# Second attention of a two-layer AdaLN kernel: projections at 0.6 to 0.8 of a round, its elementwise steps in the last fifth

## The chip, the cores and the metric

The kernel runs on one core of a Trainium2 chip. The metric is the device time of one execution in microseconds (us); the time before is 2012.13 us, the median of three runs (2011.39 to 2016.81). One further execution was profiled.

The engines are written as in the profile: PE (TensorE, matrix products; PEld are its weight loads), DVE (VectorE), ACT (ScalarE), POOL (GpSimd), SP (SyncE, which here only starts DMAs). Each engine works off its own queue in order.

## What is computed

The input is 8 sequences of 512 tokens with 128 channels. Two layers follow, each of an attention part and a feed-forward part, with layer norms, scales and gates from a condition vector. Shortened:

```python
h = layernorm(x) * (1 + ca) + sa
x = x + ga * L0_attn(h)        # 16-head causal attention and a state space scan, mixed; then a dense FFN
h = layernorm(x) * (1 + cb) + sb
x = x + gb * L0_ffn(h)         # 8 experts, 2 per token, and a shared one
h = layernorm(x) * (1 + ca) + sa
x = x + ga * L1_attn(h)        # "second attention"
h = layernorm(x) * (1 + cb) + sb
x = x + gb * L1_ffn(h)         # channel mix with the token before
```

The state space scan of layer 0 runs over 512 tokens for 256 channels and 16 states each: `h = exp(dt*A)*h + (x*dt)*B`, `y = sum_n C*h`.

The second attention (`L1_attn`) gets its axes swapped: what it treats as the sequence is the batch of 8, so that each token position attends over the 8 sequences, in 8 heads of 16 channels, without a mask. A window of 65 is padded with zeros, which adds 57 zero scores to each softmax sum:

```python
q = (x @ Wq.T + bq) * scale;  k = x @ Wk.T + bk;  v = x @ Wv.T + bv
scores[i, j, h] = sum_d q[i, h, d] * k[j, h, d]      # i, j over the 8, for each position
probs = softmax(scores with 57 zeros added)
out[i] = sum_j probs[i, j, h] * v[j]
```

## The kernel before

**Rounds.** `for b in range(NB)` (line 1285) makes eight rounds. Each traces several generators, "parts", interleaved by `weave`. A part is `(pieces, whole, begin, end)`: its pieces yield a cost, `whole` is the sum of its costs, and `weave` always advances the part whose place is lowest, where a part starts at `begin` and moves by `cost * (end - begin) / whole`. The numbers 0 to 1 are thus places in the order of one round and not times. The loop stands in a manual schedule for PE, ACT and DVE: these three engines issue in the order in which the pieces are traced. POOL and SP are ordered by the scheduler.

The parts of round b are: the rest of attention b of layer 0 (`ahead`, 0 to 1), the scan of b (`ssm_scan`, 0 to 0.83), the norm of b+1 (`head`, 0.1 to 0.55), the second attention of b-2 (`attention2`, 0 to 1, from b = 2 on), the scan's inputs for b+1 (`after`, 0.8 to 0.97), the first pieces of attention b+1 (0.85 to 1), and the FFN, routing and experts of b-1 (`behind`, 0 to 0.9). After the last round the second attention of sequences 6 and 7 runs beside the channel mix of layer 1.

**The scan** (`ssm_scan`, line 770). Sixteen units, two states by 128 channels each. DVE multiplies the input (L815), runs two scans (L820) and adds the two states (L804, in the first two units L799); POOL multiplies each scan's result by C (L823) and adds to the sum (L805, L802), in the end times the gate (L834). ACT makes the decays (L790) and starts the loads of B and C (L783). Then PE projects (L839) and DVE adds (L846).

**The scan's inputs** (`ssm_inputs`, line 684). PE L688 and L709, a convolution on DVE (L697), silu on ACT, PE L724, then for each half of the channels: PE L742, ACT L750, L751, L753, POOL L755, DVE L758, POOL L759; then ACT L765, POOL L766 and L767.

**The second attention** (`attention2`, line 316). A layer norm (`lnc` tiles: PE L256, ACT L259 and L261, PE L268, DVE L277, POOL's power at L278, PE L283, DVE L290, ACT L297). Four `kv` tiles (PE L329, two DVE sums L338 each) and one `q` tile (PE L347, DVE L354). Token positions lie on the partitions, so the rest is elementwise: in `attended` (line 360), for each of four query pairs, POOL multiplies k by q in two halves (`pr`, L377) and DVE sums over the channels (L366). DVE takes the maximum and subtracts it (L391 to L393), ACT takes two exponentials (L395, L396), DVE makes the softmax (L398 to L403). Then POOL multiplies v by the weights (`pv`, L417), DVE sums over the 8 (L408), and SP stores the result (`kept`, L432). `pr`, `pv` and the normalised input share one ring of two buffers; `k2`, `v2` and `q2` have one buffer each.

`attention2` ends with `yield from paced(attended(...))`: `paced` traces each piece so that its instructions queue behind the last marked DVE instruction of the layer 0 attention.

All the products of PE that are not attention scores or sums take their PSUM tile from one ring of three buffers (`mm_tile`, line 155).

**Other lines used below.** L544 row maxima of layer 0 attention (DVE); L563 adds them to q; L623, L635 its normalisation; L652 (ACT) and L653 (POOL) add one half of its result to h, L655 (DVE) the other; L478 its values; L582 its exponentials. Experts: L1128 gathers rows (POOL DMA), L1185 and L1211 their two products (PE), L1222 and L1223 store, L1234 gathers the results (POOL DMA), L1246, L1251, L1259, L1262 add them to x.

Of the kernel before, what the change touches and what calls it, by code (L numbers as in the profile page):

```python
# [19 lines left out]
NB = 8  # L20
# [56 lines left out]
def kernel(  # L77
# [51 lines left out]
    def crow(name):  # L129
        a, b = ROW[name]  # L130
        return row_sb[:, a:b]
# [23 lines left out]
    def mm_tile(name):  # L155
        return pmm.tile([P, 512], F32, tag="mm", name=name)
# [34 lines left out]
    def mod(l, j, b):  # L191
        return mods[l][:, j, b : b + 1]
# [35 lines left out]
    def paced(pieces):  # L228

        pieces, cost = iter(pieces), 0.0  # L230
        while cost is not None:
            if marks:
                with tc.issue_after(marks[0]):
                    cost = next(pieces, None)
            else:
                cost = next(pieces, None)
            if cost is not None:
                yield cost
# [55 lines left out]
    def layernorm(dst, src, scale, bias, name, lane, cost=0.9, n=T, ring=mm_tile, wait=0.0):  # L294

        d = yield from normalised(src, name, lane, cost, n, ring, wait)
        nc.scalar.activation(dst, d, AF.Identity, bias=bias, scale=scale)  # L297
        yield cost
# [10 lines left out]
    def cwb(name):  # L309
        lo, hi = WB[name]  # L310
        return wb_sb[:, lo:hi]

    def half(k):
        return slice(U * k, U * k + U)

    def attention2(s, at):

        hT = at.tile([P, 2, T], F32, tag="pr", name=f"hT{s}", bufs=2)[:, 0, :]
        yield from layernorm(hT, xT[:, s, :], mod(1, 1, s), mod(1, 0, s), f"lnc{s}", SECOND)

        k2 = at.tile([P, NB, C], F32, tag="k2", name=f"k2_{s}", bufs=1)
        v2 = at.tile([P, C, NB], F32, tag="v2", name=f"v2_{s}", bufs=1)
        q = at.tile([P, NQ, C], F32, tag="q2", name=f"q2_{s}", bufs=1)
        bias = crow("qkv_b").unsqueeze(1)
        for i0 in range(0, NB, 2):
            ps = mm_tile(f"kv{s}_{i0}")
            for i in range(2):
                for k in range(2):
                    nc.tensor.matmul(  # L329
                        ps[half(k), 2 * C * i : 2 * C * (i + 1)],  # L330
                        lhsT=hT[:, (i0 + i) * U : (i0 + i + 1) * U],
                        rhs=cwb("qkv")[:, C:],
                        start=True,
                        stop=True,
                    )
            both = k2, v2.rearrange("p c i -> p i c")
            for k, to in enumerate(t[:, i0 : i0 + 2, :] for t in both):
                nc.vector.tensor_add(  # L338
                    to,
                    ps.rearrange("p (i k c) -> p k i c", i=2, k=2)[:, k],  # L340
                    bias[:, :, C * (k + 1) : C * (k + 2)].to_broadcast([P, 2, C]),
                )
            yield 0.9
        ps = mm_tile(f"q2{s}")
        for i in range(NQ):
            for k in range(2):
                nc.tensor.matmul(  # L347
                    ps[half(k), C * i : C * (i + 1)],
                    lhsT=hT[:, (NQ * k + i) * U : (NQ * k + i + 1) * U],
                    rhs=cwb("qkv")[:, :C],  # L350
                    start=True,
                    stop=True,
                )
        nc.vector.tensor_add(  # L354
            q, ps.rearrange("p (i c) -> p i c", i=NQ), bias[:, :, :C].to_broadcast([P, NQ, C])
        )
        yield 0.9
        yield from paced(attended(s, at, q, k2, v2))

    def attended(s, at, q, k2, v2):  # L360

        sc = at.tile([P, NQ, NB, H1], F32, tag="sc", name=f"sc{s}", bufs=1)

        def summed(last):
            i, pr = last
            nc.vector.tensor_reduce(  # L366
                sc[:, i, :, :].rearrange("p j h -> p (j h)"),
                pr.rearrange("p j (h d) -> p (j h) d", d=D1),
                AX.X,
                ALU.add,  # L370
            )

        last = None
        for i in range(NQ):
            pr = at.tile([P, NB, C], F32, tag="pr", name=f"pr{s}_{i}", bufs=2)
            for k in range(0, NB, NQ):
                nc.gpsimd.tensor_mul(  # L377
                    pr[:, k : k + NQ, :],
                    k2[:, k : k + NQ, :],
                    q[:, i, :].unsqueeze(1).to_broadcast([P, NQ, C]),  # L380
                )
            if last:
                summed(last)
            last = i, pr
            yield 1.6
        summed(last)

        scale = float(D1) ** -0.5
        s3 = [P, NQ, NB, H1]
        mx = at.tile([P, NQ, H1], F32, tag="mx", name=f"mx{s}", bufs=1)  # L390
        nc.vector.tensor_reduce(mx, sc.rearrange("p i j h -> p i h j"), AX.X, ALU.max)  # L391
        nc.vector.tensor_scalar(mx, mx, 0.0, None, ALU.max)
        nc.vector.tensor_sub(sc, sc, mx.unsqueeze(2).to_broadcast(s3))  # L393
        yield 1.6
        nc.scalar.activation(sc, sc, AF.Exp, scale=scale)  # L395
        nc.scalar.activation(mx, mx, AF.Exp, scale=-scale)  # L396
        sm = at.tile([P, NQ, H1], F32, tag="sm", name=f"sm{s}", bufs=1)
        nc.vector.tensor_reduce(sm, sc.rearrange("p i j h -> p i h j"), AX.X, ALU.add)  # L398
        nc.vector.scalar_tensor_tensor(
            sm, mx, float(PADS), sm, op0=ALU.mult, op1=ALU.add  # L400
        )
        nc.vector.reciprocal(sm, sm)
        nc.vector.tensor_mul(sc, sc, sm.unsqueeze(2).to_broadcast(s3))  # L403
        ao = at.tile([P, NQ, C], F32, tag="ao", name=f"ao1_{s}", bufs=1)

        def gathered(last):
            i, pr = last
            nc.vector.tensor_reduce(ao[:, i, :], pr, AX.X, ALU.add)  # L408

        last = None  # L410
        for i in range(NQ):
            pr = at.tile([P, C, NB], F32, tag="pr", name=f"pv{s}_{i}", bufs=2)
            HH = H1 // 2
            s4 = [P, HH, D1, NB]
            for k in range(2):
                cs, hs = (slice(k * n, (k + 1) * n) for n in (C // 2, HH))
                nc.gpsimd.tensor_mul(  # L417
                    pr[:, cs, :].rearrange("p (h d) j -> p h d j", d=D1),
                    v2[:, cs, :].rearrange("p (h d) j -> p h d j", d=D1),
                    sc[:, i, :, hs].rearrange("p j h -> p h j").unsqueeze(2).to_broadcast(s4),  # L420
                )
            if last:
                gathered(last)
            last = i, pr
            yield 1.6
        gathered(last)
        if s == NB - 1:
            at2.append(ao)
            return
        kept = dram.tile([NB, U, C], F32, tag=f"ao{s}", name=f"kept{s}", bufs=1)  # L430
        for k in range(2):
            nc.sync.dma_start(  # L432
                out=kept[NQ * k : NQ * (k + 1)].rearrange("i u c -> u i c"), in_=ao[half(k)]
            )
        at2.append(kept)
# [10 lines left out]
    with ExitStack() as l0:  # L446
# [6 lines left out]
        a2 = l0.enter_context(tc.tile_pool(name="a2", bufs=2))  # L453
# [655 lines left out]
        def experts(b, hm, hmd, rt, ei, pos, tw, wT):  # L1109
# [154 lines left out]
            )  # L1264
            yield 2.4

        ready, inputs, routed = {}, {}, {}
        nc.sync.dma_start(out=wb_sb, in_=wb)

# [13 lines left out]
        with tc.manual_schedule(engines={mybir.EngineType.PE, mybir.EngineType.Activation, mybir.EngineType.DVE}):  # L1283
            behind = None
            for b in range(NB):
                h = ready[b][0]


                parts = [(ahead, 48.1, 0.0, 1.0)]
                parts.append((paced(ssm_scan(b, h, *inputs.pop(b))), 19.3, 0.0, 0.83))  # L1290
                if b + 1 < NB:
                    parts.append((head(b + 1), 9.5, 0.1, 0.55))
                if b >= 2:
                    parts.append((attention2(b - 2, a2), 23.4, 0.0, 1.0))
                if b + 1 < NB:
                    parts.append((after(b + 1), 8.0, 0.8, 0.97))
                    ahead = attention(b + 1)
                    parts.append((some(ahead, BEGUN), 7.3, 0.85, 1.0))
                if behind:
                    parts.append((behind, 88.8, 0.0, 0.9))  # L1300
                weave(*parts)
                behind = finish(b, h)
# [9 lines left out]
            LAST = NB - 1  # L1312
# [129 lines left out]

            def through(sp):

                yield from attention2(sp, a2)
                fetched(0)


# [37 lines left out]
            def closed(k):  # L1486
# [24 lines left out]
                yield 0.9  # L1511

            weave(
                (attention2(LAST, a2), 23.4, 0.0, 1.0),
                *(
                    (pair(i, (MIX, REST)), 23.4, 0.15 + 0.45 * k, 0.7 + 0.45 * k)
                    for k, i in enumerate(range(SHARE, NB, 2))
# [145 lines left out]
```

## Time and profile before

| | |
|---|---|
| median of 3 runs | 2012.13 us |
| profiled execution | 2025.32 us |
| its span, first to last instruction | 2023.6 us |
| busy: PE, DVE, POOL, ACT | 1545.1, 1373.5, 1184.1, 1027.1 us |
| mean granted TensorE clock | 0.831 |
| DMA | 170.67 MB, 84 GB/s |

The profile page gives each engine's busy time and groups of instructions by line with their mean duration, and what ended the idle time ahead of them. The timeline lists instructions in order of time. The windows view gives the busy time of each engine in stretches that the reader cuts; cut at the rounds, it compares a round with another one. In slices of a fortieth of the span, the busy tenths repeat with the rounds (about 222 us, four to five slices):

```profile
DVE  1698577747894789658884779468875778262155
POOL 1577355835685558755775658654875568542241
```

The instructions of the second attention, over all eight sequences:

```profile
L366 DVE TENSOR_REDUCE sc<-pr 128x64 f32<-128x1024 f32 x32 | 38.5, 1204 | 0.5 <-POOL pr L377 0.5
L408 DVE TENSOR_REDUCE ao<-pv 128x128 f32<-128x1024 f32 x32 | 38.3, 1198 | 0.0
L329 PE MATMUL kv<-wb_sb,hT 128*64 128x256 f32 x256 | 39.7, 441 | 0.0
```

Read: line, engine, operation, output and inputs with shapes, count; then busy us in all, mean ns of one, and the idle time ahead of them with what ended it.

### The profile page before, as it was taken

Reading aid. Unit: us, or ns where it says so; the run is one execution under the profiler, and the core shown is the slowest. Engines: PE = TensorE matmul, PEld = TensorE weight load, DVE = VectorE, ACT = ScalarE, POOL = GpSimd, SP = SyncE. Lnnn points to the kernel's source line nnn. Section 1 sums busy time; section 2 is a strip of 40 time slices with the busy share of each in tenths; the row PEclk is TensorE's granted clock in tenths of the full one; section 3 lists DMA queues with packets and bytes.
Section 4 is the critical chain, followed back from the end, with each engine's and each line's share of the span. In section 5 each row is a group of like instructions: output and inputs, shape, how many; then the busy total and the mean of one; then the engine's idle time right before and its main releaser. Section 6 shows DMA issues by size and latency. Waiting matters only on the chain. (4 is left out here: it accounts for less than half of the span.)

```text
span 2023.6 us, 28511 instructions
## 1 busy us (share of the span) xinstructions
PE 1545.1 (76%) x10210; PEld 936.9 (46%) x10210; DVE 1373.5 (68%) x1760; ACT 1027.1 (51%) x1852; POOL 1184.1 (59%) x853
## 2 busy tenths in 40 slices
PE   5665788888778868888778777886977777857764
PEld 3332344644455435544554445543554345535642
DVE  1698577747894789658884779468875778262155
ACT  2432545754565637554565547553746455324432
POOL 1577355835685558755775658654875568542241
PEclk9776878988888879888898878887988888768876
DMA  2211013612351216312450225212441135204400
GB/s 98 70 63 42 33 63 104 185 35 73 88 165 50 73 56 182 86 53 66 113 163 18 89 61 167 79 49 74 142 122 49 58 105 155 60 8 129 112 16 18
DMA packets 100750, 170.67 MB, mean 84 GB/s; under 512 B 12665, under 2 KB 47617, under 8 KB 100481
## 3 DMA queue, kind: packets, MB, share of 16 engines
q1 hardware_dynamic: 75776, 87.14, 15.0%
q10 hardware_dynamic: 18720, 69.09, 10.3%
q0 software_dynamic: 6112, 12.62, 3.3%
q8 instruction: 81, 1.33, 0.3%
q14 instruction: 61, 0.49, 0.1%
HBM read 154.39 MB, written 14.42 MB: 83 GB/s over the span
## 5 line engine op out<-in xcount | busy, mean ns | idle before, releaser
L823 POOL TENSOR_TENSOR hs<-hs,bc 128x512 f32<-128x512 f32 x256 | 393.4, 1539 | 312.0 <-DVE hs L820 221.6
L820 DVE TENSOR_TENSOR_SCAN hs<-da,hs 128x512 f32<-128x512 f32 x256 | 418.0, 1635 | 6.7
L582 ACT ACTIVATE ex<-e 128x768 f32<-128x768 f32 (+1 forms) x192 | 158.9, 881 | 191.8 <-PE e L520 175.7
L544 DVE TENSOR_REDUCE mpad<-s 128x2 f32<-128x256 f32 (+3 forms) x256 | 195.4, 814 | 66.6 <-PE s L520 66.0
L805 POOL TENSOR_TENSOR xc<-xc,hs 128x512 f32<-128x512 f32 x112 | 191.3, 1708 | 40.1 <-DVE hs L804 32.7
L815 DVE TENSOR_TENSOR hs<-bc,dtw 128x1024 f32<-128x1024 f32 x128 | 200.3, 1565 | 18.0 <-DMA bc<-bc 13.3
L512 PE MATMUL e<-qT,kT 32*128 32x512 f32 (+3 forms) x1024 | 136.4, 579 | 89.2 <-DVE mpad L544 46.0
L1128 POOL DMA_INDIRECT xg<-hmd,rt_sb x120 | 149.8, 1248 | 73.7 <-PE xs L1140 26.1
L790 ACT ACTIVATE da<-dtu,own 128x512 f32<-128x512 f32 x256 | 169.0, 717 | 2.0 <-POOL dtu L766 1.2
L1194 ACT ACTIVATE eh<-e,we 128x128 f32<-128x128 f32 x480 | 132.4, 380 | 61.0 <-PE e L1185 56.2
L1185 PE MATMUL e<-xs_sb,we 128*128 128x128 f32 x960 | 141.4, 304 | 24.5 <-DVE ln_d L290 12.4
L1185 PEld LDWEIGHTS e<-xs_sb,we 128*128 128x128 f32 x960 | 129.5, 213 | 34.7 <-issue 14.5
L804 DVE TENSOR_TENSOR hs<-hs 128x512 f32<-128x512 f32 x112 | 115.2, 1029 | 33.8 <-POOL hs L823 33.8
L512 PE MATMUL s<-kT,qT 32*128 32x128 f32 (+3 forms) x1024 | 126.5, 520 | 9.0 <-ACT ex L582 4.1
L1211 PE MATMUL e<-we,eh 128*128 128x128 f32 x960 | 122.3, 281 | 13.7 <-ACT eh L1194 13.6
L417 POOL TENSOR_TENSOR pv<-v,sc 128x512 f32<-128x512 f32 x64 | 96.5, 1535 | 55.0 <-DVE ao L408 34.9
L520 PEld LDWEIGHTS <-ident_b 128*128 128x128 bf16 x1024 | 63.9, 104 | 134.7 <-issue 129.0
L1211 PEld LDWEIGHTS e<-we,eh 128*128 128x128 f32 x960 | 115.7, 196 | 21.8 <-ACT eh L1194 20.4
L512 PEld LDWEIGHTS e<-qT,kT 32*128 32x128 f32 x1024 | 54.1, 217 | 140.3 <-issue 91.2
L596 PE MATMUL av<-ex,va 128*32 128x512 f32 (+3 forms) x1024 | 110.8, 523 | 1.4 <-ACT ex L582 1.3
L377 POOL TENSOR_TENSOR pr<-k,q 128x512 f32<-128x512 f32 x64 | 82.9, 1321 | 18.3 <-DVE q L354 15.3
L1234 POOL DMA_INDIRECT yg<-ys,pos x64 | 61.0, 953 | 36.0 <-issue 14.6
(327 smaller groups left out, 2974.6 us busy)
## 6 DMA issues: line engine op xcount, KB each, us to landing
bc<-bc ACTq DMA_DIRECT2D x128, 512.0 KB
we<-in_w_dram SPq DMA_DIRECT2D x120, 258.0 KB
we<-in_w_dram SPq DMA_DIRECT2D x120, 256.0 KB
ys<-y SPq DMA_DIRECT2D x56, 128.0 KB
we_None<-in_w_dram SPq DMA_DIRECT2D x8, 258.0 KB
xin<-in_x_dram SPq DMA_DIRECT2D x8, 256.0 KB
we_None<-in_w_dram SPq DMA_DIRECT2D x8, 256.0 KB
hmd<-hmt_sb SPq DMA_DIRECT2D x8, 256.0 KB
```

Of the source, the lines that this page charges most:

```text
L512: nc.tensor.matmul(tiles[i // 2][:, i % 2, c0 : c0 + n], lhsT=lhs[quadrant(i)], rhs=rhs[quadrant(i)], start=True, stop=False,)
L544: nc.vector.tensor_reduce(mpad[:, qi, 2 * pr : 2 * pr + 2, HD : HD + 1], tiles[pr][:, :, a : a + n], AX.X, ALU.max, negate=True,)
L582: nc.scalar.activation(t[:, :, :c0], tiles[pr][:, :, :c0], AF.Exp)
L790: nc.scalar.activation(da[:, n, :], dt[c], AF.Exp, scale=A_sb[:, c, n0 + n : n0 + n + 1])
L805: nc.gpsimd.tensor_add(y, y, hs[:, 0, :])
L815: nc.vector.tensor_mul(hs, bcs[n0][0], dtx[c].unsqueeze(1).to_broadcast([P, NN, T]))
L820: nc.vector.tensor_tensor_scan(hs[:, n, :], da[:, n, :], hs[:, n, :], 0.0, ALU.mult, ALU.add)
L823: nc.gpsimd.tensor_mul(hs[:, n, :], hs[:, n, :], bcs[n0][1][:, n, :])
L1128: nc.gpsimd.indirect_dma_start(out=xg, out_offset=None, in_=hmd[:, :], in_offset=bass.IndirectOffsetOnAxis(ap=rt[:, k : k + 1], axis=0),)
L1185: nc.tensor.matmul(ps[:, m * P : (m + 1) * P], lhsT=we1[:, m * P : (m + 1) * P], rhs=xs[:, i, :], start=True, stop=True,)
L1194: nc.scalar.activation(t[:, m, :], ps[:, m * P : (m + 1) * P], AF.Silu, bias=we1[:, FF + m : FF + m + 1],)
L1211: nc.tensor.matmul(ps[:, i * C : (i + 1) * C], lhsT=hid[i][:, m, :], rhs=w2s[i][:, m * C : (m + 1) * C], start=(m == 0), stop=(m == NFF - 1),)
```

## The change

`attention2` no longer runs `attended` itself. It leaves the paced generator in a list, and a new generator `summed_up` runs it. In rounds 2 to 6 the two become parts of their own: the norm and projections (cost 9.0) from 0.6 to 0.8, and the elementwise rest (cost 14.4) from 0.82 to 1.0. In the last round and after it `whole2` runs one after the other at the places that `attention2` had. No computation changes.

```diff
@@ attention2
         yield 0.9
-        yield from paced(attended(s, at, q, k2, v2))
+        waiting.append(paced(attended(s, at, q, k2, v2)))
+
+    waiting = []
+
+    def summed_up():
+
+        yield from waiting.pop()
@@
+        def whole2(s):
+
+            yield from attention2(s, a2)
+            yield from summed_up()
@@ the rounds
-                if b >= 2:
-                    parts.append((attention2(b - 2, a2), 23.4, 0.0, 1.0))
+                if b + 1 == NB:
+                    parts.append((whole2(b - 2), 23.4, 0.0, 1.0))
+                if 2 <= b < NB - 1:
+                    parts.append((attention2(b - 2, a2), 9.0, 0.6, 0.8))
+                    parts.append((summed_up(), 14.4, 0.82, 1.0))
@@ through
-                yield from attention2(sp, a2)
+                yield from whole2(sp)
@@ after the rounds
-                (attention2(LAST, a2), 23.4, 0.0, 1.0),
+                (whole2(LAST), 23.4, 0.0, 1.0),
```

## Prediction

> **What bounds the kernel now.** Read first the page's busy row and groups, then the timeline for the moments at which rounds begin, then the windows view cut there.
>
> ```profile
> PE 1545.1 (76%) x10210; PEld 936.9 (46%) x10210; DVE 1373.5 (68%) x1760; ACT 1027.1 (51%) x1852; POOL 1184.1 (59%) x853
> L823 POOL TENSOR_TENSOR hs<-hs,bc 128x512 f32<-128x512 f32 x256 | 393.4, 1539 | 312.0 <-DVE hs L820 221.6
> L820 DVE TENSOR_TENSOR_SCAN hs<-da,hs 128x512 f32<-128x512 f32 x256 | 418.0, 1635 | 6.7
> L417 POOL TENSOR_TENSOR pv<-v,sc 128x512 f32<-128x512 f32 x64 | 96.5, 1535 | 55.0 <-DVE ao L408 34.9
> L377 POOL TENSOR_TENSOR pr<-k,q 128x512 f32<-128x512 f32 x64 | 82.9, 1321 | 18.3 <-DVE q L354 15.3
> ```
>
> No engine is full; the limit must be sought by stage. I count a round from the first L815 of a scan to the next round's. T0 is the end of L834, which closes the scan. Round 1 (244.8 to 449.2) has no second attention; rounds 2 to 6 have it and take 221.6 to 222.2 us each. Windows of round 1 and round 4, each cut at T0 (columns: us, then PE, PEld, DVE, ACT, POOL busy, clock):
>
> ```profile
> 244.80:400.30 155.50, 127.30 (x895) 78.25 (x896) 122.53 (x154) 91.82 (x168) 103.83 (x71) 0.84 0.40 116
> 400.30:449.20 48.90, 41.92 (x281) 22.22 (x279) 18.29 (x27) 29.93 (x48) 17.75 (x18) 0.90 0.14 41
> 893.10:1061.60 168.50, 132.03 (x943) 83.74 (x943) 141.85 (x175) 94.09 (x173) 115.85 (x80) 0.86 0.39 112
> 1061.60:1114.90 53.30, 45.39 (x294) 24.22 (x294) 23.33 (x33) 29.79 (x47) 29.90 (x26) 0.87 0.10 29
> ```
>
> So the second attention costs 221.8 - 204.4 = 17.4 us a round: 13.0 in the scan, 4.4 in the tail. In the scan DVE is the bound (141.9 of 168.5 us, and 69 of 74 us in 979 to 1053). Part of it is DVE's own work, part lies in this moment:
>
> ```profile
> 1014.63 6.47 DVE L820 TENSOR_TENSOR_SCAN hs<-da,hs 128x512 f32<-128x512 f32 x1
> ...
> 1017.50 2.50 POOL L377 TENSOR_TENSOR pr<-k,q 128x512 f32<-128x512 f32 x2
> ```
>
> The scan lasts 1.22 us in the median, here 6.47, until POOL's run of products ends at 1020. In the tail no engine is full; it is a chain of short steps, whose end is:
>
> ```profile
> 1102.46 1.26 POOL L759 TENSOR_TENSOR dtu<-dtu,dte 128x512 f32<-128x512 f32 x1 [1.00 <-DVE dte L758]
> ...
> 1109.42 1.48 DVE L758 SCALAR_TENSOR_TENSOR dte<-dtw,dte 128x512 f32<-128x512 f32 x1
> ...
> 1111.01 0.81 ACTq L783 DMA_DIRECT2D bc<-bc  x2
> ...
> 1114.90 1.23 DVE L815 TENSOR_TENSOR hs<-bc,dtw 128x1024 f32<-128x1024 f32 x1 [2.27 <-DMA bc<-bc]
> ```
>
> The next scan begins 3.9 us after L783, which stands behind the second L758; POOL works 9.3 of the 14.1 us from 1100.84 on.
>
> **The change, part by part.** Rounds 2 to 6 alone differ; rounds 0, 1, 7 and the closing keep their order. No instruction is added or removed (ACT's five table loads at L395 become five at L582). The built order of each engine shows where things land. Below, dtw_0 is the round's first L755 on POOL.
>
> *1. Scan, what leaves.* Eight L377 on POOL (9.99 us), four L366 (4.8) and L391 to L393 (1.6) on DVE, and the projections' early part. If nothing of the attention were left, the scan would be round 1's: 155.5 us.
>
> *2. Scan, what comes in late.* Normalisation and first kv tile now stand before the last scan: PE L256 1.2, L268 1.0, L283 1.1, L329 1.5 = 4.8 us; POOL's power L278 1.9 between scan products. Also the PSUM ring of three tiles: L261 frees the first tile only after two ACT copies, and the next "den" matmuls wait about 3.2 us for it. Nothing of it on the path: 0, since PE idled 7.7 of the 58 us before T0 in round 1. All of it: 4.8 + 3.2 = 8.0. Placing the instructions by hand into round 1's timeline, the last scan but one slips 3.7, the last one starts behind the kv sums, and T0 slips **3.4**. I take that: 158.9 us instead of 168.5, a gain of 9.6.
>
> *3. T0 to L688 (the next round's inputs).* Now 8.8 us (1061.6 to 1070.4), in round 1 4.9. Before it stand three kv tiles and q. The third tile needs a PSUM buffer that is freed by the second's sums, and those stand on DVE behind the last L804, 3.9 us before T0. From there: L804 0.7, sums 1.0, kv 1.5, transposes 0.9, L1211 2.05, kv 1.5, scores with mask 1.5, L1185 1.1, q 2.0, L839 1.9, L1211 1.1 = 15.25, minus 3.9 = **11.3**. Lower bound 8.8 (the kv work fills waits that PE has there now), upper 14 (PE stalls once more for a tile). L653, now ahead of the last L805 on POOL, is inside the hand placement. L1234 comes 4 us after L688 as now: it waits for the expert rows' DMA, and the two pr products before it (5.1 us) are done by then.
>
> *4. L688 to dtw_0.* 30.4 now, 30.0 in round 1, where the eight pv products are missing: they don't set it. Two L366 fall into DVE's waits for PE (3.2 us at 1081). I keep **30.3**.
>
> *5. dtw_0 to the next scan.* Now 14.1 us (1100.84 to 1114.9). New in ACT's queue: L395 and L396 (0.42 + 0.21) between the two halves of L750 to L753; ACT waits 2.41 us for PE there, which hides them as long as L393 is done. L1262 ends at 1093.94, 6.9 us before dtw_0; two L366 (2.4) and L391 to L393 (1.6) behind it end 2.9 before; ACT gets there 0.5 after. New in DVE's queue: L398 to L403 ahead of L623 and L758; undisturbed 0.60 + 0.19 + 0.35 + 0.42 = 1.6 us, ending 2.9 after dtw_0. New in POOL's queue: all eight L417 between the steps that lead to the scan. From 2.9 on POOL runs pv_0 3.04, L759 1.27, pv_1 3.04, L755 0.62, pv_2 3.04, L766 and L767 2.54, pv_3 3.04 = 16.6 without a hole; then L408 1.2 and L563 0.7 on DVE stand before L815: 21.4, and eight new hand-overs between engines at some 0.15 us (L755's end to L758's start is 1101.46 to 1101.64) make it **22.6**. Lower bound: the pv products (12.2 us) minus POOL's holes now (14.1 - 9.3 = 4.8): 21.5. Upper: DVE's sums and POOL's products stretch each other as in the row above, 26. Queued behind: hs_0_1's L815 waits for the last L767, which ends about 23.5 after dtw_0, before its turn. SP's two kept DMAs (0.63 us each) go some 10 us later, between L736 and the next xin as before, whose issue is 23 us off.
>
> *Sum:* 158.9 + 11.3 + 30.3 + 22.6 = 223.1 against 221.8 now: **+1.3 us a round, +6.5 in five**; the hand-overs in step 3 are not counted singly, 0.3 a round for them (two at 0.15 that nothing covers): +1.6, **+8 us**. The profiled execution lies at 2025.32 us (span 2023.6 and 1.7 around it), 13 above the median of 2012.13; I carry the difference over: **2020**. The scan's gain of 9.6 is real and is given back by a longer tail.
>
> A rule of the Trainium skill stands beside the 6.47 us row. The row shows DVE held until POOL's run ends. "SBUF — State Buffer", section "SBUF: two separate sides", says that DVE and GpSimd share one port pair, taken as an exclusive lock for a whole instruction, so that the loser fully blocks. By it all 9.99 us of L377 come back, with DVE's 6.4 us: 16.4 a round; round 1 against round 4 shows that 13.0 is all there is. It also speaks against the change: the lock is taken again by eight L417 beside the DVE steps that start the scan.
>
> **The rivals.** *Faster.* The late projections vanish in PE's idle time, so that the scan returns nearly all of its 13.0 us (156 instead of 158.9), and L688 comes 10 us after T0: 156 + 10 + 30.3 + 22.3 = 218.6, -3.2 a round, -16 in all: 1996. For it: PE is busy only 127 of 155.5 us in round 1's scan. Against: PE is full in the last third, and the ring of three tiles ties each kv tile to a DVE sum. It decides as soon as the tail grows by less than the scan gives back.
>
> *No change.* Steps 2 to 5 come out 1.3 us a round shorter: within 6 us of 2012. For it: both sides of the sum are near 10 us.
>
> *Much slower.* The softmax part is late: L366 of pr_3 and L391 to L393 slip past dtw_0, L395 then stops ACT in front of the second L750, and with it L765, L783 and the scan. It decides once L393 ends more than 3.4 us later than I place it; from there each us costs one. At 8 us late, +4.6 more a round: 5 x 6.2 = +31, 2043. Against: the last L366 needs only pr_3, and POOL is done with it 19 us after L688 (4 to L1234, eight of those at 1.25, pr_2 and pr_3 5.1), 11 before dtw_0.
>
> *It doesn't do what it says.* The build shows the pr, pv and sums moved; only "0.6 to 0.8" is inexact, as three kv tiles and q land behind the last scan. That is in step 3.
>
> **How the numbers follow.** A run can tell 0.3% (6 us) from no change. Forecast (slower by 6 to 20 us) 0.42, much slower 0.13, no change 0.17, faster 0.28. Slower together 0.55. The likeliest gives 2020, its own range 2018 to 2032. For 8 in 10 I go to the faster rival with a little of step 5's lower bound, 1993, and to the much slower one, 2043.
>
> **What would show it.** In the changed profile: scan windows of 157 to 161 us in rounds 2 to 6 and few L820 above 2.5 us (step 1, 2); T0 to L688 of 11 us, with waits of PE for DVE's kv sums (step 3); L417 among L755 to L767 and 22 us from the first L755 to L815 (step 5); ACT not waiting at L395. I am wrong if the tail grows by less than 9 us, if L815 still follows 14 us after L755, or if the scan doesn't shrink.

## The result, and the profile after

The changed kernel takes **2019.22 us** (median of 18 runs, 2013.24 to 2027.37), the kernel before 2012.91 us beside it (18 runs, 2008.75 to 2020.55). The ratio is 1.0035, with a 95% interval of 1.0024 to 1.0046: slower by about 6 us. The interval excludes no change, but the difference is half of what the kernel before moves from one session to another (last section). The prediction was 2020.

In the changed kernel's code every line behind the edit in `attention2` stands 6 lower: L366 is now L372, L377 L383, L417 L423, L688 L694, L755 L761, L815 L821, L820 L826, L823 L829. The text below keeps the old numbers for stages and names both where a profile is shown. The page of the changed kernel, busy row and the groups that answer to those of before:

```profile
PE 1559.2 (77%) x10210; PEld 932.0 (46%) x10210; DVE 1345.8 (67%) x1760; ACT 1024.5 (51%) x1852; POOL 1183.1 (59%) x853
L829 POOL TENSOR_TENSOR hs<-hs,bc 128x512 f32<-128x512 f32 x256 | 391.1, 1531 | 282.6 <-DVE hs L826 180.2
L826 DVE TENSOR_TENSOR_SCAN hs<-da,hs 128x512 f32<-128x512 f32 x256 | 393.5, 1540 | 8.1 <-ACT da L796 0.5
L383 POOL TENSOR_TENSOR pr<-k,q 128x512 f32<-128x512 f32 x64 | 82.3, 1316 | 66.0 <-DVE q L354 63.2
L423 POOL TENSOR_TENSOR pv<-v,sc 128x512 f32<-128x512 f32 x64 | 98.7, 1565 | 33.8 <-DVE sc L409 19.5
```

The instruction counts are those of before. DVE is busy 27.7 us less, of which the scans (L826) give 24.5: their mean fell from 1635 to 1540 ns. POOL's `pr` and `pv` no longer run beside them in rounds 2 to 6: in the kernel before the 14 scans that overlap one of them took 3.53 us in the mean, the other 242 took 1.53. Still the time did not fall. The page can't say why; the windows can. Round 1 (without the second attention) and round 5 (with it), each cut at T0; columns as in the prediction:

```profile
246.40:400.60 154.20, 123.52 (x898) 76.71 (x899) 124.21 (x154) 92.71 (x170) 104.05 (x71) 0.87 0.40 120
400.60:452.60 52.00, 43.97 (x275) 23.09 (x274) 17.57 (x26) 29.00 (x46) 17.61 (x18) 0.84 0.10 30
1115.70:1275.40 159.70, 128.22 (x900) 78.76 (x900) 125.87 (x160) 92.16 (x169) 107.94 (x73) 0.84 0.38 112
1275.40:1337.00 61.60, 52.24 (x339) 27.85 (x337) 32.13 (x47) 31.44 (x50) 37.12 (x33) 0.80 0.14 39
```

The scan went from 168.5 to 159.7 us with DVE 16 us less busy in it, and the tail from 53.3 to 61.6 us. What was taken out of one stretch came back in the other.

The means over rounds 2 to 6, from three profiles of each kernel (the first of each, then those of the experiments below):

| stage, us | predicted | before | after |
|---|---|---|---|
| scan, to T0 | 158.9 | 168.5, 168.4, 168.1 | 158.9, 158.7, 158.5 |
| T0 to L688 | 11.3 | 8.8, 8.8, 8.8 | 11.5, 12.0, 12.6 |
| L688 to dtw_0 | 30.3 | 30.5, 30.7, 30.5 | 29.4, 29.2, 29.5 |
| dtw_0 to the next L815 | 22.6 | 14.1, 14.1, 13.9 | 21.6, 21.5, 21.5 |
| round | 223.1 | 221.9, 222.0, 221.3 | 221.4, 221.4, 222.1 |
| rounds 0 and 1 together | as before | 374.4, 372.4, 371.9 | 380.0, 375.3, 373.3 |
| last T0 to the end | as before | 298.1, 300.0, 294.9 | 291.2, 294.3, 296.3 |
| span | | 2023.6, 2024.3, 2015.4 | 2017.3, 2017.5, 2018.8 |

The first profile of the changed kernel showed 17.5 and 17.6 us from dtw_0 to L815 in rounds 0 and 1 too, where nothing was changed. Its second and third profile have 15.3 and 13.9, and 15.2 and 13.8, so that was one execution and not the change.

These lengths go with the TensorE clock that was granted in the stretch. In round 1, whose instructions no run changed, dtw_0 to L815 took 13.7 to 14.0 us where the mean clock there was 0.88 to 1.00, 15.9 and 16.1 us at 0.79, and 17.4 to 17.6 us at 0.74 (14 profiles). In rounds 2 to 6 that stretch had 1.00 in every profile of the kernel before and 0.58 to 0.74 in every one of the changed kernel. Why the clock is granted lower there was not found.

Where the 11 us between T0 and L688 lie is seen in the timeline of PE and DVE at the end of round 5's scan (T0 is 1275.4, L688, now L694, comes at 1286.5):

```profile
1273.77 1.97 PE L329 MATMUL kv<-wb_sb,hT 128*64 128x256 f32 x8 [4.28 <-DVE v L338]
...
1279.34 1.08 PE L329 MATMUL kv<-wb_sb,hT 128*64 128x256 f32 x8
...
1282.70 1.09 PE L347 MATMUL q<-wb_sb,hT 128*64 128x128 f32 x16
...
1275.78 0.43 DVE L338 TENSOR_TENSOR k<-kv,row_sb 128x256 f32<-128x256 f32 x1 [2.16 <-PE kv L329]
...
1280.47 0.42 DVE L338 TENSOR_TENSOR k<-kv,row_sb 128x256 f32<-128x256 f32 x1 [2.96 <-PE kv L329]
```

PE stood 4.28 us for the DVE sums of the kv tile before (its PSUM buffer). At T0 the third kv tile is being computed, and the fourth and q are still to come. They go ahead of L694 in PE's queue, which waits only 0.4 us more up to there. The stretch varies with the granted clock as well: over the three profiles of the changed kernel it took 9.6 us in the one round at 1.00, and 12.6 to 13.2 at 0.76 to 0.78.

Behind dtw_0 (L761 at 1315.41) the timeline of POOL and DVE shows the second half of what was moved:

```profile
1315.41 0.62 POOL L761 TENSOR_SCALAR dtw<-dte 128x512 f32<-128x512 f32 x1 [4.05 <-ACT dte L757]
1318.14 3.42 POOL L423 TENSOR_TENSOR pv<-v,sc 128x512 f32<-128x512 f32 x2 [2.12 <-DVE sc L409]
1321.52 1.27 POOL L765 TENSOR_TENSOR dtu<-dtu,dte 128x512 f32<-128x512 f32 x1
1322.74 3.00 POOL L423 TENSOR_TENSOR pv<-v,sc 128x512 f32<-128x512 f32 x2
1325.71 0.62 POOL L761 TENSOR_SCALAR dtw<-dte 128x512 f32<-128x512 f32 x1
1326.30 3.00 POOL L423 TENSOR_TENSOR pv<-v,sc 128x512 f32<-128x512 f32 x2
...
1332.30 2.98 POOL L423 TENSOR_TENSOR pv<-v,sc 128x512 f32<-128x512 f32 x2
...
1317.57 0.43 DVE L409 TENSOR_TENSOR sc<-sc,sm 128x256 f32<-128x256 f32 x1
...
1318.08 0.63 DVE L764 SCALAR_TENSOR_TENSOR dte<-dtw,dte 128x512 f32<-128x512 f32 x1
...
1335.31 1.22 DVE L414 TENSOR_REDUCE ao<-pv 128x128 f32<-128x1024 f32 x1 [2.98 <-POOL pv L423]
...
1337.05 1.88 DVE L821 TENSOR_TENSOR hs<-bc,dtw 128x1024 f32<-128x1024 f32 x1
```

All four pairs of `pv` run between the two L761, L765 and their like that lead to the scan; POOL has no hole from 1318 on, and the last sum of `pv` (L414) and one L569 (L563 before) stand on DVE ahead of the scan's L821.

### The profile page after: what moved, and what is told of

It reads as the page before. It is cut to its first block, busy times and chain, and to the rows that moved or that the text cites. A ratio compares the mean times of both kernels' runs of the same rounds, so it can differ in the third digit from the quotient of the medians.

```text
span 2017.3 us, 28485 instructions
## 1 busy us (share of the span) xinstructions
PE 1559.2 (77%) x10210; PEld 932.0 (46%) x10210; DVE 1345.8 (67%) x1760; ACT 1024.5 (51%) x1852; POOL 1183.1 (59%) x853
## 4 chain that ended last, share of the span: by engine, by line
PE 41%; DVE 32%; POOL 10%; ACT 8%; issue 5%; DMA 3%; SPq 0%; ACTq 0%; DVEq 0%; POOLq 0%
DVE hs L826 8%; DVE hs L821 6%; DVE mpad L550 5%; POOL pv L423 3%; POOL hs L829 3%; PE s L518 3%; PE e L518 3%; PE e L1217 2%; PE av L602 2%; DVE hs L810 2%; PE e L1191 2%; PE e L1161 2%; DMA we<-in_w_dram 1%; PE rt L1096 1%; PE f L882 1%
## 5 line engine op out<-in xcount | busy, mean ns | idle before, releaser
L829 POOL TENSOR_TENSOR hs<-hs,bc 128x512 f32<-128x512 f32 x256 | 391.1, 1531 | 282.6 <-DVE hs L826 180.2
L826 DVE TENSOR_TENSOR_SCAN hs<-da,hs 128x512 f32<-128x512 f32 x256 | 393.5, 1540 | 8.1 <-ACT da L796 0.5
L550 DVE TENSOR_REDUCE mpad<-s 128x2 f32<-128x256 f32 (+3 forms) x256 | 195.6, 816 | 53.2 <-PE s L526 52.6
L821 DVE TENSOR_TENSOR hs<-bc,dtw 128x1024 f32<-128x1024 f32 x128 | 218.8, 1709 | 6.3 <-DMA bc<-bc 6.3
L1134 POOL DMA_INDIRECT xg<-hmd,rt_sb x120 | 144.3, 1202 | 71.3 <-PE xs L1146 23.2
L518 PE MATMUL e<-qT,kT 32*128 32x512 f32 (+3 forms) x1024 | 128.6, 558 | 42.5 <-DVE mpad L550 28.3
L1191 PE MATMUL e<-xs_sb,we 128*128 128x128 f32 x960 | 130.2, 287 | 21.6 <-DMA we<-in_w_dram 12.2
L518 PE MATMUL s<-kT,qT 32*128 32x128 f32 (+3 forms) x1024 | 137.6, 555 | 6.5 <-ACT ex L588 4.1
L1217 PE MATMUL e<-we,eh 128*128 128x128 f32 x960 | 129.9, 291 | 11.3 <-ACT eh L1200 9.1
L810 DVE TENSOR_TENSOR hs<-hs 128x512 f32<-128x512 f32 x112 | 103.6, 925 | 44.4 <-POOL hs L829 44.4
L1191 PEld LDWEIGHTS e<-xs_sb,we 128*128 128x128 f32 x960 | 117.8, 197 | 32.1 <-issue 13.9
L1217 PEld LDWEIGHTS e<-we,eh 128*128 128x128 f32 x960 | 120.5, 202 | 23.5 <-ACT eh L1200 19.4
L383 POOL TENSOR_TENSOR pr<-k,q 128x512 f32<-128x512 f32 x64 | 82.3, 1316 | 66.0 <-DVE q L354 63.2
L423 POOL TENSOR_TENSOR pv<-v,sc 128x512 f32<-128x512 f32 x64 | 98.7, 1565 | 33.8 <-DVE sc L409 19.5
L1240 POOL DMA_INDIRECT yg<-ys,pos x64 | 61.3, 957 | 35.0 <-issue 16.5
```

The costliest lines, as they stand in the source:

```text
L423: nc.gpsimd.tensor_mul(pr[:, cs, :].rearrange("p (h d) j -> p h d j", d=D1), v2[:, cs, :].rearrange("p (h d) j -> p h d j", d=D1), sc[:, i ...
L518: nc.tensor.matmul(tiles[i // 2][:, i % 2, c0 : c0 + n], lhsT=lhs[quadrant(i)], rhs=rhs[quadrant(i)], start=True, stop=False,)
L550: nc.vector.tensor_reduce(mpad[:, qi, 2 * pr : 2 * pr + 2, HD : HD + 1], tiles[pr][:, :, a : a + n], AX.X, ALU.max, negate=True,)
L821: nc.vector.tensor_mul(hs, bcs[n0][0], dtx[c].unsqueeze(1).to_broadcast([P, NN, T]))
L826: nc.vector.tensor_tensor_scan(hs[:, n, :], da[:, n, :], hs[:, n, :], 0.0, ALU.mult, ALU.add)
L829: nc.gpsimd.tensor_mul(hs[:, n, :], hs[:, n, :], bcs[n0][1][:, n, :])
```

## The experiments

Each run is a change of the changed kernel unless said otherwise. Kernels of one session (one group of runs) ran on the same chip with the kernel before beside them; since the kernel before did not take the same time in all sessions (last section), ratios are compared, and the tables of rounds.

### The kernel before, profiled again

No edit.

> The kernel before, once more, for a second profile of it. If the 221.9 us of rounds 2 to 6 belong to the kernel, they come again within 1 us, and an execution near the median of 2013 us differs from the first profile (2025 us) in other places or by the same factor everywhere. If one profile is not to be trusted to 1%, the rounds differ by more than 2 us.

Span 2024.3, rounds 2 to 6 within 0.5 us of the first profile: the stage table of before is a property of the kernel. Beside this group of runs its median was 2025.66 us (13 runs), not 2012.9.

### Projections early, the elementwise part as changed

```diff
-                    parts.append((attention2(b - 2, a2), 9.0, 0.6, 0.8))
+                    parts.append((attention2(b - 2, a2), 9.0, 0.0, 0.385))
                     parts.append((summed_up(), 14.4, 0.82, 1.0))
```

> Only the elementwise part stays late; norm and projections go back to 0 to 0.385 of the round, about where they were before. My theory: the late kv tiles and the PSUM ring lengthen T0 to L688 from 5 to 11.5 us; without them it is 5 to 7, the scan stays near 159 (3 us for norm and kv sums, now early), L755 to L815 stays 21.5: a round of 216 to 217 instead of 221.4, so 20 to 27 us less than the changed kernel, near 1995. Rival: the stretch after T0 is long because POOL and DVE do the elementwise part there, whatever PE does: T0 to L688 stays above 10 and the time stays within 8 us of the changed kernel's.

1992.43 us, ratio 0.9846 (0.9816 to 0.9876). Windows of round 4 in this run, scan and tail:

```profile
880.40:1039.10 158.70, 131.81 (x961) 82.08 (x962) 130.21 (x166) 94.06 (x172) 113.07 (x76) 0.87 0.38 115
1039.10:1094.90 55.80, 44.21 (x279) 21.97 (x277) 28.89 (x42) 29.60 (x48) 33.29 (x30) 0.85 0.12 38
```

The scan stays where the change had brought it, with 61 more matmuls in it, and T0 to L688 falls to 4.6 us in the mean of rounds 2 to 6 (11.5 to 12.6 in the changed kernel); dtw_0 to L815 stays at 21.5. Rounds take 215.1. The late kv tiles cost some 7 us a round in the tail and buy about 1 us in the scan (159.6 against 158.5 to 158.9). T0 to L688 had a granted clock of 1.00 in all five rounds here; against the one round of the changed kernel at 1.00 the difference is 5 us.

### Without the products of v

```diff
-            for k in range(2):
+            for k in range(2 * (s > NB - 4)):
@@
-            last = i, pr
+            last = i, pr if s > NB - 4 else v2
```

The eight L417 of each of the sequences 0 to 4 are left out; DVE sums `v2` itself in their place.

> The changed kernel without the eight L417 products for sequences 0 to 4 (DVE sums v itself in their place, so the output of the second attention is wrong for them). My theory: the products stand in POOL's queue between the steps that lead to the next scan; without them L755 to L815 falls from 21.5 to 15 to 16.5 us (the softmax on DVE still delays L623 and L758), everything else stays: 5 to 6.5 us a round, 25 to 32 us in all, near 1990. Rival: the softmax steps on DVE and ACT set this stretch: it stays at 19 or more, and the time falls by less than 12 us.

2007.38 us, ratio 0.9919 (0.9893 to 0.9945); rounds of 218.4, and dtw_0 to L815 18.8 us. That is between the theory and the rival, and nearer to the rival: of the 7.5 us by which that stretch had grown, the products of `pv` make only 2.7. Timeline of DVE and POOL in that run's round 4 (dtw_0 is 1087.90):

```profile
1087.90 0.62 POOL L761 TENSOR_SCALAR dtw<-dte 128x512 f32<-128x512 f32 x1 [4.05 <-ACT dte L757]
...
1096.11 0.62 POOL L761 TENSOR_SCALAR dtw<-dte 128x512 f32<-128x512 f32 x1 [3.50 <-ACT dte L757]
...
1088.72 0.61 DVE L404 TENSOR_REDUCE sm<-sc 128x32 f32<-128x256 f32 x1 [1.47 <-ACT sc L401]
...
1090.56 0.63 DVE L764 SCALAR_TENSOR_TENSOR dte<-dtw,dte 128x512 f32<-128x512 f32 x1
```

POOL has holes now, but the softmax (L404 to L409) stands on DVE ahead of L764 (L758 before): it waits 1.47 us for ACT's exponential, and L764 starts 2.0 us after L761's end where it was 0.2 us before (1101.46 to 1101.64). The second L761 follows 8.2 us after the first. So two chains share this stretch, and taking the products on POOL away uncovers the other, which runs over PE. PE in that run's round 4, and then in round 4 of the kernel before (dtw_0 at 1100.84):

```profile
1090.70 1.93 PE L634 MATMUL rb<-cst_sb,rd 128*32 128x128 f32 x32 [2.06 <-DVE rd L629]
1092.57 2.07 PE L748 MATMUL dt<-xd_sb,dtw_sb 8*128 8x512 f32 x2
1094.57 3.78 PE L649 MATMUL ao<-at,wa_sb 128*128 128x512 f32 x4
...
1101.51 1.08 PE L628 MATMUL rb<-cst_sb,rd 128*32 128x128 f32 x32
1102.52 1.12 PE L742 MATMUL dt<-xd_sb,dtw_sb 8*128 8x512 f32 x2
1103.57 2.25 PE L643 MATMUL ao<-at,wa_sb 128*128 128x512 f32 x4
```

L634 (L628 before) waits for the reciprocal L629, which stands behind the softmax on DVE: it starts 2.8 us after dtw_0 where it was 0.7. From there on the granted clock is 0.50, where the kernel before had 1.00, and these three groups and the scores behind them take 3.7 us longer. The second L764 comes behind them and is itself 0.8 us shorter. So of the remaining 4.8 us the softmax ahead of L629 makes some 2 us and the lower clock the larger part. Whether the clock would stay up without that wait was not tried.

### The products of v in the next scan's start

```diff
+                if b >= 3:
+                    parts.append((held.pop(), 6.4, 0.0, 0.2))
                 if b + 1 == NB:
-                    parts.append((whole2(b - 2), 23.4, 0.0, 1.0))
+                    parts.append((whole2(b - 2), 23.4, 0.2, 1.0))
                 if 2 <= b < NB - 1:
-                    parts.append((attention2(b - 2, a2), 9.0, 0.6, 0.8))
-                    parts.append((summed_up(), 14.4, 0.82, 1.0))
+                    parts.append((attention2(b - 2, a2), 9.0, 0.25, 0.55))
+                    parts.append((scored(), 8.0, 0.82, 1.0))
```

(`scored` runs the generator up to the softmax's subtraction and hands the rest to `held`.)

> Products with q late as in the change (0.82 to 1), products with v at 0 to 0.2 of the next round, where DVE has idle time in the scan's start, and the projections at 0.25 to 0.55. My theory: L755 to L815 near 15 to 17, T0 to L688 5 to 7, the scan 160 to 164 (norm and kv sums 3, pv beside the scan's start up to 5): a round of 211 to 217, a time of 1970 to 1997. Rival: pv in the scan's start holds DVE as the pr products did later in it (13 us a round for both in before): the scan goes back to 166 or more and the time is 2005 or more.

2015.91 us, ratio 0.9954 (0.9930 to 0.9977). The rival held: in rounds 3 to 6 dtw_0 to L815 is 16.6 to 19.9, and the scan is back at 168.0 to 168.5, where round 2, which has no `pv` in it, takes 159.1. What was moved to the scan's start (the exponentials, the rest of the softmax, the products and their sums) costs about 9 us there; the run moves them together, so what the products alone cost is not shown. POOL at the start of round 4 of this run:

```profile
885.33 4.76 POOL L423 TENSOR_TENSOR pv<-v,sc 128x512 f32<-128x512 f32 x2 [2.83 <-DVE sc L409]
890.05 4.44 POOL L829 TENSOR_TENSOR hs<-hs,bc 128x512 f32<-128x512 f32 x2
...
895.48 6.40 POOL L423 TENSOR_TENSOR pv<-v,sc 128x512 f32<-128x512 f32 x4
901.85 2.18 POOL L829 TENSOR_TENSOR hs<-hs,bc 128x512 f32<-128x512 f32 x1
```

The first pair takes 4.76 us beside the scan (3.0 undisturbed), and the scan's L829 stands behind it.

### The changed kernel, profiled again

No edit.

> The changed kernel itself once more, for a second profile. Its rounds 2 to 6 took 221.4 us on average in the first profile (scan 158.9, T0 to L688 11.5, L688 to dtw_0 29.5, dtw_0 to L815 21.5), 0.4 below the kernel before, and rounds 0 and 1 took 3.7 and 1.9 us longer than before, with 17.6 us from dtw_0 to L815 although nothing of the change stands there. Theory (the small loss in the medians sits in the rounds, some 1 us each): rounds 2 to 6 of 222 to 224 in this profile, rounds 0 and 1 as before. Rival (it sits in rounds 0 and 1 and is built in): these are 170 + 3.7 and 204.4 + 2 again, rounds 2 to 6 again 221.4. Ratio 1.002 to 1.005 in either.

2020.23 us, ratio 1.0054 (1.0031 to 1.0076). Rounds 2 to 6 took 221.4 again, and rounds 0 and 1 are back at 170.9 and 204.4. Neither held: the loss is not in rounds 0 and 1, and rounds 2 to 6 do not lie above those in the profiles of before.

### Projections early and the elementwise part earlier: three places

```diff
-                    parts.append((attention2(b - 2, a2), 9.0, 0.6, 0.8))
-                    parts.append((summed_up(), 14.4, 0.82, 1.0))
+                    parts.append((attention2(b - 2, a2), 9.0, 0.0, 0.385))
+                    parts.append((summed_up(), 14.4, 0.76, 0.94))
```

The other two have 0.79 and 0.97, and 0.79 and 0.91. In the run with 0.82 to 1.0 POOL was idle for 11 us ahead of dtw_0, so there was room for `pv`, if only the softmax came in time.

> Projections at 0 to 0.385 (as in the run with a ratio of 0.985) and the elementwise part at 0.79 to 0.97 instead of 0.82 to 1.0: in DVE's order the third and fourth sum of pr and the maximum then stand ahead of L1262 and L544, and the first pv sum ahead of L544. Theory (POOL lies idle for 11 us before dtw_0 while the softmax waits its turn on DVE, so the pv products can run there): two of the four pairs of pv are done before dtw_0, dtw_0 to L815 16 to 18 instead of 21.5, scan as before it 158.7 to 160.6, rounds of 209 to 211, ratio 0.970 to 0.975. Rival (the DVE queue, not POOL, sets the tail, so a sum that waits for POOL ahead of L544 gives all back): L688 to dtw_0 grows by 3 or more, rounds of 214 to 216, ratio 0.985.

1971.09 us, ratio 0.9804 (0.9776 to 0.9831). dtw_0 to L815 fell to 14.9, but L688 to dtw_0 rose to 35.4: half theory, half rival; rounds of 212.4.

> Projections at 0 to 0.385, the elementwise part at 0.76 to 0.94: the first sum of pr stands right behind L563 of the last scan units, the softmax ahead of L478 and L635, two pv sums ahead of L544. Theory: all pv products but one are done before dtw_0, dtw_0 to L815 14 to 15, L688 to dtw_0 29 to 31, scan up to 1.5 longer by one pr product among the last L823; rounds of 208 to 210, ratio 0.965 to 0.97. Rival (products of the second attention beside the last scan units and the convolution L697 stretch what they lie beside): scan 162 or more or T0 to L688 7 or more, rounds of 212 to 216.

**1953.68 us, ratio 0.9724 (0.9697 to 0.9751)**, rounds of 207.9: 157.8 scan, 4.3, 29.8, and 16.0 from dtw_0 to L815. The theory held but for 1 to 2 us in the last stretch, and the ratio came out just above the 0.965 to 0.97 that was said. That stretch had a granted clock of 0.74 to 0.91; with the same placement the one round at 1.00 (round 5 of the run with all rounds, below) took 13.9 us. POOL around dtw_0 of this run's round 4:

```profile
1037.89 0.98 POOL L1240 DMA_INDIRECT yg<-ys,pos  x1 [0.30 <-issue]
1040.46 5.96 POOL L423 TENSOR_TENSOR pv<-v,sc 128x512 f32<-128x512 f32 x4 [1.59 <-DVE sc L409]
1048.22 5.97 POOL L423 TENSOR_TENSOR pv<-v,sc 128x512 f32<-128x512 f32 x4 [1.80 <-DVE ao L414]
...
1054.27 0.62 POOL L761 TENSOR_SCALAR dtw<-dte 128x512 f32<-128x512 f32 x1
1055.77 1.27 POOL L765 TENSOR_TENSOR dtu<-dtu,dte 128x512 f32<-128x512 f32 x1 [0.88 <-DVE dte L764]
```

All eight products lie in the hole between the expert rows (L1240) and dtw_0. Compare the stretch in the changed kernel above: there they begin 2.7 us behind dtw_0.

> Projections at 0 to 0.385, the elementwise part at 0.79 to 0.91: begins as late as the run at 0.79 to 0.97, but packed: all four sums of pr by the end of L697, all four pv sums ahead of L544. Theory: dtw_0 to L815 14, but L544 and with it L623 and the second L758 now stand behind a pv sum that waits for POOL, so L688 to dtw_0 is 30 to 33; rounds of 208 to 212. Rival (DVE's waits ahead of L544 cost as much as the pv products behind dtw_0 did): rounds of 213 or more.

2004.10 us, ratio 0.9991 (0.9966 to 1.0015): the rival, with rounds of 217.8. The scan is as short as in the best run (157.5), dtw_0 to L815 16.8, but L688 to dtw_0 takes 39.3 us. DVE in the round at 1050 shows why:

```profile
1063.21 1.22 DVE L372 TENSOR_REDUCE sc<-pr 128x64 f32<-128x1024 f32 x1 [3.39 <-POOL pr L383]
1068.11 1.22 DVE L372 TENSOR_REDUCE sc<-pr 128x64 f32<-128x1024 f32 x1 [3.68 <-POOL pr L383]
...
1076.07 1.22 DVE L414 TENSOR_REDUCE ao<-pv 128x128 f32<-128x1024 f32 x1 [2.21 <-POOL pv L423]
...
1085.89 1.22 DVE L414 TENSOR_REDUCE ao<-pv 128x128 f32<-128x1024 f32 x1 [2.01 <-POOL pv L423]
1087.03 1.94 DVE L550 TENSOR_REDUCE mpad<-s 128x2 f32<-128x256 f32 x4
```

DVE waits four times for POOL, 11.3 us in all, with L484, L629 and L641 of the layer 0 attention and the row maxima L550 (L478, L623, L635 and L544 before) queued behind. The chain goes on over PE, which waits for L629; here, and then in the best run:

```profile
1070.87 1.93 PE L634 MATMUL rb<-cst_sb,rd 128*32 128x128 f32 x32 [7.98 <-DVE rd L629]
...
1038.27 1.08 PE L634 MATMUL rb<-cst_sb,rd 128*32 128x128 f32 x32 [1.24 <-DVE rd L629]
```

The wait is 6.7 us longer here, and L688 to dtw_0 is 8.9 us longer in this round (9.5 in the mean). In the best run L550 starts 30.6 us after T0, here 41.0. The stretch also had a lower granted clock (0.82 here, 0.99 in the best run's round 4), which is not told apart. The same instructions, begun 0.03 of a round later and packed, cost 10 us a round.

### The pair on one chip

> The kernel before, profiled on the same chip as the changed kernel in the next run. Two earlier profiles of it had spans of 2023.6 and 2024.3, while its median was 2012.9 and 2010.3 us where the changed kernel's was 2019.2 and 2020.2 (ratios 1.0035 and 1.0054). Theory (chips differ by some 0.7 per cent, and the change does cost about 1.5 us a round on one and the same chip): in this pair rounds 2 to 6 of before are 1 to 2 us shorter than those of the changed kernel. Rival (the rounds are equal, the loss sits in rounds 0 and 1 or in the closing): rounds 2 to 6 agree within 0.5 us in the mean and the loss shows elsewhere.

> The changed kernel beside the run before, on the same chip: rounds 2 to 6 of 221 to 222 us as in its two profiles (221.4 in the mean in both). The theory and its rival are told apart by the difference of the two tables; one execution is uncertain by some 5 us in all, 1 us a round.

Before 2017.15 us, after 2020.52 us, one execution each; rounds 2 to 6 are 221.3 and 222.1 in the mean. That looks like the theory, but all of the difference lies in round 2 (219.1 against 223.1); rounds 3 to 6 sum to 887.4 in both. And in that session the 17 runs of before have a median of 2024.34, with the changed kernel's one run below it. The pair doesn't settle it.

### The best placement in the last round too

```diff
-                if b + 1 == NB:
-                    parts.append((whole2(b - 2), 23.4, 0.0, 1.0))
-                if 2 <= b < NB - 1:
+                if b >= 2:
```

(on top of the run with 0.76 to 0.94)

> The best placement so far (projections at 0 to 0.385, elementwise part at 0.76 to 0.94, ratio 0.972) given to the last round too, where the second attention of sequence 5 ran as a whole over 0 to 1. Theory (the last scan has the same contention on DVE and POOL: 165.6 us against 156.5 to 158.7 in rounds 2 to 6): the last scan falls to 157 to 159, and since no next round's inputs follow it, the elementwise part runs beside the channel mix: 4 to 8 us less in all, ratio 0.968 to 0.971. Rival (after the last scan POOL is needed by the closing, which then starts later): the closing of 293 us grows by as much, ratio 0.972 or more.

1954.99 us, ratio 0.9656 (0.9627 to 0.9684). The ratio is better only because the kernel before was slower beside these runs (2024.34 against 2010.25). The tables decide: the last scan fell from 165.6 to 155.5, and the closing grew from 293.2 to 302.6 us. The rival held. (Round 1, which this edit does not touch, took 211.3 us in this execution and 201.4 in the other, with 37.4 and 30.2 us from L688 to dtw_0 at a granted clock of 0.77 and 0.89. Without it the two spans differ by 0.8 us.)

### Projections late, but ahead of the last scan units

```diff
-                    parts.append((attention2(b - 2, a2), 9.0, 0.0, 0.385))
+                    parts.append((attention2(b - 2, a2), 9.0, 0.45, 0.65))
```

(on top of the run with 0.76 to 0.94)

> Elementwise part at 0.76 to 0.94 as in the best run, projections at 0.45 to 0.65 instead of 0 to 0.385: late in the scan, but with the last kv tile and q ahead of the last scan units instead of behind them. Theory (T0 to L688 was long in the changed kernel because three kv tiles and q land behind the last scan, not because they are late): T0 to L688 4 to 5, scan 157 to 160, rounds of 206 to 210, ratio 0.970 to 0.975. Rival (PE is full in the last third of the scan, so projections there delay it wherever they end): scan 161 or more or T0 to L688 8 or more, rounds of 212 or more, ratio above 0.98.

2023.05 us, ratio 0.9994 (0.9975 to 1.0013). T0 to L688 is 5.7 us, near the 4 to 5 of the theory, but the scan takes 169.8: the rival. The waits of DVE in round 4's scan (waiting for: us in all, times, longest):

```profile
DVE k L338 <- PE kv L329: 8.2, 4, 4.7
DVE hs L810 <- POOL hs L829: 3.7, 1, 3.7
```

In the best run no wait for a kv tile is among the listed waits of the same stretch. Up to the eleventh scan unit the two run alike (its L821 starts 101.2 us into the scan, against 103.5 in the best run); from there to the fifteenth unit this one needs 42.0 us instead of 28.3. PE is late with the kv tiles, and the scan's next instructions stand behind their sums in DVE's queue. The granted clock was lower as well (0.83 from 1000 to 1030 here, 1.00 from 970 to 1000 in the best run); its share in PE's lateness is not told apart.

## Why the prediction was right, point by point

**Scan, what leaves and what comes in late (158.9):** measured 158.5 to 158.9. L826 above 2.5 us: none in rounds 2 to 6, as was to be seen. The split of 13.0 less and 3.4 more is not shown: with the projections early the scan is 159.6, so the moved elementwise work makes nearly the whole gain, and the projections cost the scan about as much early as late.

**T0 to L688 (11.3):** 11.5 to 12.6. The cause given, kv tiles and q in PE's order behind the last scan, is shown by the run with early projections: 4.6. The share of the PSUM ring is not told apart from the tiles' own time. The clock, which no term had, moved the stretch from 9.6 to 13.2 us between rounds.

**L688 to dtw_0 (30.3):** 29.2 to 29.5, 1 us too long. That it is not set by the second attention holds only in this order; the run at 0.79 to 0.91 made it 39.3.

**dtw_0 to L815 (22.6):** 21.5 to 21.6 in every round, which is the sum without the 1.2 us for hand-overs. It is also the stated lower bound, but by chance: POOL is busy 8.8 of the 14.1 us in the kernel before and not 9.3, which makes that bound 21.0. L393 ends 3.3 ahead of dtw_0 and L403 2.6 behind it (2.9 and 2.9 predicted), and ACT does not wait at L395. The makeup was mis-sized, though. By the prediction POOL's run was the bound and the softmax only its start; without the products 4.8 of the 7.5 us remained, so there is a second chain, 2.7 us shorter than the first: the softmax on DVE ahead of L623, and PE behind it at a granted clock of 0.50, a price that the prediction did not have.

**The sum (+1.3, with hand-overs +1.6 a round):** this step is not confirmed. The three profiles of each kernel give rounds of 221.7 before and 221.6 after in the mean; the last two terms came out about 1 us short each. So as far as the profiles show, that 2020 was met is luck: by these tables the forecast would have been no change. The difference of 8 us was added to the median of 2012.13 and not to the profiled execution. That execution (2025.32) lies above all 18 runs of before that were measured beside the changed kernel, while the changed kernel's profiles (2019.1, 2019.3, 2020.5) lie in the middle of its runs. So the loss of 6 us (10 in the second session) is measured against executions of before that none of its profiles shows. Where the loss lies and what is shorter in them stays open: all three profiles of before lie at 2017 us or more, none near 2010 to 2013.

**The rivals.** Faster: its condition, that PE's late projections vanish in idle time, is refuted by the 4.28 us wait and by T0 to L688. No change: by the rounds of the profiles alone this is what happened. Much slower: L393 stayed 3.3 us ahead of dtw_0; the run with `pv` in the next scan shows L393 9 to 13 us behind it, but there L395 was moved too, so that condition was not tried by itself.

**The rule beside the 6.47 us row.** The Trainium skill's page "SBUF — State Buffer", section "SBUF: two separate sides", lets an operation of DVE with two SBUF inputs and one of POOL that reads SBUF exclude each other for a whole instruction. In the changed kernel's round 5 the scan's L826, L821 and L810 take 46.8, 27.4 and 13.3 us, in round 4 of the kernel before 52.0, 24.1 and 16.2: 4.8 us less in all, against 8.8 us that the scan gained. The rest is put down to work that left the scan's queues; no run took the two apart. So of the 9.99 us of `pr` that the prediction, by the rule, let come back to DVE, about half did. Its warning for the tail came true at a small price: the two L764, with two inputs, took 0.63 and 0.68 us, and it was POOL that took longer beside them, 3.42 us for the pair of `pv` that began at 1318.14 (3.00 for the next) and 1.74 for L773 at 1330.59 (1.26 undisturbed). The scan's first L821, begun beside POOL's L772, took 1.88 us and not 1.23.

## What to carry to other kernels

Moving work behind a critical stretch pays only if a hole of the right engine lies there and every producer arrives before it: the same elementwise part cost 7.5 us a round behind dtw_0 and about 2 in POOL's hole ahead of it (none in the one round at full clock), and a shift of 0.06 of a round took the time from 1.5% below the kernel before to 2.8% below it, once the projections had gone back to the scan's first half. Under a hand-written order, read for each placement which instruction of the critical chain is queued behind the wait: one consumer set ahead of its producer costs the wait and what is queued behind it (with 8.2 us of such waits the scan was 12 us longer, with 11.3 us the stretch to dtw_0 was 9.5 longer, both at a lower granted clock too). Compare the granted clock of a stretch in both profiles before its length is put down to a queue. And sum a prediction against the profiled execution as well as against the runs: if the two differ by more than the effect, the profile may not show the case that the runs measure.

## What the runs showed of the hardware

Within a round the granted TensorE clock goes between 0.50 and 1.00, and matrix products follow it: the pair L742 took 1.12 us in the kernel before at 1.00, and the same pair (L748) 2.07 us in the run without the products of v at 0.50. A stretch whose instructions are unchanged differed by almost 4 us between executions, and was longer where its clock was lower (round 1, dtw_0 to L815, 13.7 us at 1.00 and 17.6 us at 0.74).

The kernel before had medians of 2012.9, 2025.7, 2010.3 and 2024.3 us in four sessions, on at least three different chips, and was shorter where its granted clock was lower: 0.818 to 0.828 at 2010.3, 0.826 to 0.835 at 2025.7. The changed kernel stayed at 2019.2, 2020.2 and 2020.5 us (the last a single execution) at a clock of 0.815 to 0.824. So between sessions a kernel's place can move by 0.7%, twice what this change is worth, and not every kernel moves alike. The cause was not found.
